# Linear attention and a mixture of experts on one core: zero fills copied in memory, weight preparation re-spaced, some row normalisation moved to ScalarE

## The chip, the core and the metric

The kernel runs on one core of a Trainium2 chip. The metric is the device time of one execution in microseconds (us), a median over several runs. A core has a matrix engine (TensorE, PE in the profile), a vector engine (VectorE, DVE), a scalar engine (ScalarE, ACT), a general engine (GpSimd, POOL) and an engine that mostly issues transfers (SyncE, SP). Each works through its own instructions in order and waits on semaphores that others raise. Transfers are moved by 16 DMA engines; in this kernel they are issued from SP's queue (hardware-generated, q1 in the profile) and from POOL's (software-generated, q0).

## The reference

The input is x with 2048 rows of 512 columns. Cut to what matters:

```python
# attention, 32 heads of 64 columns
q = relu(ln(x) @ Wq); k = relu(ln(x) @ Wk); v = ln(x) @ Wv
kv = einsum('bhsd,bhse->bhde', k, v)
key_sum = k.sum(axis=2)
out = einsum('bhsd,bhde->bhse', q, kv) / clip(einsum('bhsd,bhd->bhs', q, key_sum), 1e-6)
x = x + out @ Wo + bo
# experts: 8, the best 2 of each row, hidden width 352
scores = ln(x) @ gate_w.T + gate_b + bias
gates = softmax(top_2(scores))
h = silu(einsum('td,ehd->teh', ln(x), w1) + b1)
x = x + sum over the row's 2 experts of gate * (h @ w2 + b2)
```

`ln` subtracts the mean of a row and divides by the square root of its variance plus 1e-5.

## The kernel before, in words

Rows come in 16 tiles of 128 (`NT`), the 2048 inner columns of the attention in four quarters of 512 (`NQ`). A wide product is split for precision: every operand is held as a rounded upper half and the rest (`split`, L163 and 164: a cast on ScalarE, then a subtraction on VectorE unless another engine is named), and `mm3` (L156) makes three matmuls of each product.

**First half, `a_step(s)`, s = 0 to 63, quarter j and row tile t.** `a_k` makes k for one row tile (12 matmuls, a relu on ScalarE, two VectorE operations, one of which adds to the key sum `kacc`); `a_g` multiplies it by the normalised rows of the step before (12 matmuls) into four accumulators. In the first quarter the rows are also loaded, normalised (`norm`, L218), transposed and split, one row tile ahead of `a_k` (`a_norm`), and written to memory (`xnd`); in later quarters `a_xn` reads them back. At t = 2 of the next quarter `a_kv` turns the accumulators into the quarter's kv matrix, stores it (`kvd`), and makes the key sums for all partitions (`ksb`). The first half also prepares weights with `raw_load` (an SP load into a ring of four buffers) and `raw_split` (the cast and the subtraction): the next quarter's k weights, four parts at t = 9 to 12; this quarter's v weights, four parts at t = 13 and 14; in the last quarter the first q weights at t = 10 to 13; and all of w1 in 22 parts, one in each of the steps 16 to 37, staged and written to memory as `w1d`. Some subtractions of the first quarter are put on POOL.

**Second half, s = 0 to 63 again.** `b_q` makes q (12 matmuls and a relu), `b_n` divides by the key-sum product, `b_t` transposes, `b_o` multiplies by the quarter's matrix M = kv @ Wo (12 matmuls, `po`), and `b_add` adds to the row kept in memory (`x1d`). `b_w` and `b_m` build the next quarter's M in four parts, and wq parts are split at t = 5 to 8. `b_x1` loads a row two steps ahead; in the first quarter POOL adds `bo`. At step 1 of the second half the last kv matrix is made and stored, read back and turned into M before the first `b_o`. In the last of these quarters the rows are normalised again, scored, and scattered by expert into the table `xs_d` (blocks of 128 rows of 515 words).

**Zeros.** `xs_d` must hold zero rows, with -1 and a row number beside them, wherever no row is scattered: 136 blocks written by `b_fill` in the second half, three a step, from two SBUF buffers, plus 7 spare blocks. The 31 blocks of `out` after the result's own rows must be zero too, since rows for the second expert are added there. In the first quarter POOL issues those 31 blocks, the spare blocks, and a copy of three experts' w2 to memory (`w2d`); all of these go through `Late` (L600), which lets them start after the relu of step 1.

**Experts.** 37 tiles of gathered rows (`c_x` loads, `c_t` transposes and splits, `c_h` first product, `c_ht` transposes, `c_y` second product). `y_out` scales by the gate on ScalarE into a buffer of the same ring of four that `raw_load` uses, and POOL scatters and adds it to `out` in memory. When all tiles that could hold second-expert rows of a row tile are through (`last_of`, plus a lag of two), `merge(t)` adds that block of `out` to the result's rows, memory to memory; what isn't merged by the end is merged after the last tile.

**Order.** From the second half's last quarter on the program's order on TensorE, VectorE, ScalarE and SP is the written one (`manual_schedule`). Before that a scheduler orders the instructions by simulated times, and `hold(held, behind)` (L166) makes instructions start only after another has ended; `k_done[s]` is the relu of `a_k(s)`, `q_done[s]` that of `b_q(s)`.

Of the kernel before, what the change touches and what calls it, by code (L numbers as in the profile page):

```python
# [26 lines left out]
def linear_attention__then__moe_kernel(  # L27
# [113 lines left out]
    xs_d = dram.tile([(NB + SPARE) * P, CX], FP, name="xs_d")  # L141
    xs_b = xs_d.rearrange("(b p) c -> b p c", p=P)
    hd = dram.tile([NTT, P, HF], FP, name="hd")
    E2 = 3
# [73 lines left out]
    def norm(xt, dst):  # L218
        sm = const.tile([P, 16], FP, tag="sm", bufs=3, name="sm")
        st, mv, sd, rs = sm[:, 0:6], sm[:, 6:8], sm[:, 8:9], sm[:, 9:10]  # L220
        first = nc.vector.bn_stats(st, xt)
        nc.vector.bn_aggr(mv, st)
        root = nc.scalar.activation(sd, mv[:, 1:2], AF.Sqrt, bias=eps)
        nc.vector.reciprocal(rs, sd)
        last = nc.vector.tensor_scalar(dst, xt, mv[:, 0:1], rs, ALU.subtract, ALU.mult)
        return first, root, last
# [84 lines left out]
    def a_kv(j):  # L311

        for p0 in range(0, PP, 2):
            pkv = aux_bank("pkv").rearrange("p (a l b) -> p a l b", a=2, l=2)
            for p in range(p0, p0 + 2):
                for c in range(CC):
                    w, g = slot_n[0][:, c], slot_n[1][:, c]
                    nc.tensor.matmul(
                        pkv[:, p - p0], w[:, 0, ts(p, P)], g[:, :, ts(p, P)],
                        start=c == 0, stop=False,  # L320
                    )
                    nc.tensor.matmul(
                        pkv[:, p - p0, 0, :], w[:, 1, ts(p, P)], g[:, 0, ts(p, P)],
                        start=False, stop=c == CC - 1,
                    )
# [12 lines left out]
        ksb[j] = fpb.tile([P, QW], FP, tag="ksb", bufs=NQ, name="ksb")  # L338
        nc.scalar.copy(ksb[j], pks)
# [3 lines left out]
    q_done = {}  # L343

    def b_x1(s):
        j, t = divmod(s, NT)
        x1s[s] = fpb.tile([P, C], FP, tag="x1", bufs=4, name="x1")
        if j == 0:
# [3 lines left out]
            nc.gpsimd.tensor_add(x1s[s], x1s[s], bo_b)  # L352
# [147 lines left out]
    zeros = []  # L500

    def b_fill(s):

        if s == 0:
            for _ in range(2):
                zeros.append(temp())
                for i0, i1, v in ((0, C + 1, 0.0), (C + 1, C + 2, -1.0)):
                    hold([nc.gpsimd.memset(zeros[-1][:, i0:i1], v)], q_done[s])
        e, k = divmod(s, -(-SB // 3))
        rows = zeros[e % 2]  # L510
        if k == 0:
            to = float(2 * S + (SPARE + e) * P)
            nc.gpsimd.tensor_scalar(rows[:, C + 2 : CX], part, to, None, ALU.add)
        for n in range(3 * k, min(3 * k + 3, SB)):
            hold([nc.gpsimd.dma_start(xs_b[e * SB + n], rows)], q_done[s])  # L515
# [21 lines left out]
    n_w1 = W1N // 512  # L537
    NC = 2
    k_done = {}

    def a_step(s):
# [11 lines left out]
        if t == 8 and j + 1 < NQ:  # L553
            for c in range(CC):
                hold([raw_load(("k", j + 1, c), wk[ts(c, P), ts(j + 1, QW)])], k_done[s - 1])
        if t in (9, 10, 11, 12) and j + 1 < NQ:
            c = t - 9
            w = slot_s[(j + 1) % 2]
            raw_split(
                ("k", j + 1, c), w[:, c, 0, :], w[:, c, 1, :], nc.vector if j else nc.gpsimd  # L560
            )
        if t == 9 and j == NQ - 1:
            for c in range(CC):
                raw_load(("q", 0, c), wq[ts(c, P), ts(0, QW)])
        if t in (10, 11, 12, 13) and j == NQ - 1:
            c = t - 10
            raw_split(("q", 0, c), slot_s[0][:, c, 0, :], slot_s[0][:, c, 1, :])
        if t == 12:
            for c in range(CC):
                raw_load(("v", j, c), wv[ts(c, P), ts(j, QW)])  # L570
        if t in (13, 14):
            for c in (2 * t - 26, 2 * t - 25):
                raw_split(
                    ("v", j, c), slot_n[0][:, c, 0, :], slot_n[0][:, c, 1, :],
                    nc.vector if j else nc.gpsimd,
                )

        w = s - NT
        if 0 <= w < n_w1:
            if w == 0:  # L580
                hold([raw_load(("w1", 0), w1[:, ts(0, 512)])], k_done[s - 1])
# [3 lines left out]
            if w + 1 < n_w1:  # L585
                hold([raw_load(("w1", w + 1), w1[:, ts(w + 1, 512)])], k_done[s - 1])
# [3 lines left out]
        if j and t == 2:  # L590
            a_kv(j - 1)

# [71 lines left out]

    zero = temp()
    pool.memset(zero[:, 0 : C + 1], 0.0)
    pool.memset(zero[:, C + 1 : C + 2], -1.0)
    for b in range(NT + NZ):
        pool.dma_start(out[S + b * P : S + (b + 1) * P, :], zero[:, 0:C])
    for b in range(SPARE):  # L670
        pool.tensor_scalar(zero[:, C + 2 : CX], part, float(2 * S + b * P), None, ALU.add)
        pool.dma_start(xs_b[NB + b], zero)
    for e in range(E2):
        pool.dma_start(w2d[e, 0:HF].bitcast(FP), w2[e])
        pool.dma_start(w2d[e, HF : HF + 1].bitcast(FP), b2[e : e + 1, :])
# [23 lines left out]

    for s in range(NC, NQ * NT):  # L700
        a_step(s)
    b_x1(0)
# [156 lines left out]
    for s in range(NS - NT):  # L859
# [4 lines left out]
        b_fill(s)  # L864
# [16 lines left out]
        if t == 4:  # L881
# [9 lines left out]
        if t in (10, 11, 12, 13):  # L891
            b_w(j + 1, t - 10)
            b_m(j + 1, t - 10)
# [190 lines left out]
    for i in range(H1):  # L1084
# [38 lines left out]
    last_of = {  # L1123
        t: max(min(F1 + 2 * t + E, 2 * (G1 - 1) + E), 2 * t + E) for t in range(NT)
    }
# [27 lines left out]
    for n, i in enumerate(y_order):  # L1153
# [5 lines left out]
        if n == H1 - 1:  # L1159
            c_h(H1)  # L1160
            c_next(H1 + 2)
# [4 lines left out]
    for i in range(H1, NE):  # L1166
# [78 lines left out]
```

## Time and profile before

| | |
|---|---|
| runs shown (3) | 1022.0 to 1026.01 us, median 1024.93 us |
| the profiled execution | 1016.79 us, of which the span is 1015.1 us |
| mean granted TensorE clock | 0.993 of full speed |
| first half, second half, experts (about) | 0 to 393, 393 to 830, 830 to 1015 us |
| DMA, mean | 210 GB/s; SP's queue 129.83 MB, POOL's 82.19 MB |
| POOL, fills of `xs_d` in the second half (L515) | 136 issues, 545 ns each |
| POOL, zero blocks of `out` (L600) | 31 issues, 557 ns each |
| ScalarE, casts of weight parts (L164) | 86, 621 ns each |
| VectorE, their subtractions (L164) | 77, 708 ns each; 9 more on POOL, 1286 ns each |
| VectorE, normalising a row (L225) | 16, 652 ns each |
| ScalarE, a row with scale and bias (L243) | 16, 816 ns each |

The profile is one execution recorded by the hardware. A row of a group gives how many instructions it has and the mean duration of one; a timeline row gives start, duration, engine, line and operation, and in brackets how long the engine sat idle before it and what ended that. A row of busy time by stretches gives for each engine the busy microseconds and the number of instructions. Matmuls of TensorE overlap, so their durations add up to more than their time: distances from start to start and counts say how fast it goes.

### The profile page before, as it was taken

What the parts mean: (1) busy time and instruction counts of PE and PEld (TensorE: products, weight loads), DVE (VectorE), ACT (ScalarE), POOL (GpSimd) and SP (SyncE); (2) the same over time, 40 slices, a digit from 0 to 9 for tenths busy, and PEclk for the clock granted to TensorE, in tenths of its full rate; (3) what the DMA queues carried; (4) which work ended last, traced back from release to release, by engine and by line L of the source; (5) the groups of instructions that cost most, each with busy time, mean ns of one, the idle gap of its engine ahead of it and who ended that gap; (6) DMA issues with size and microseconds to landing.
All of it is one profiled execution on the core that took longest, in us unless ns stands there. A gap on an engine that the chain in (4) does not pass through costs nothing. (4 is left out here: it accounts for less than half of the span.)

```text
span 1015.1 us, 14856 instructions
## 1 busy us (share of the span) xinstructions
PE 987.5 (97%) x4902; PEld 823.7 (81%) x4902; DVE 560.2 (55%) x1380; ACT 344.7 (34%) x677; POOL 260.8 (26%) x357
## 2 busy tenths in 40 slices
PE   8999999999999999999999999999999999999994
PEld 5878887788888888788788888887888789889993
DVE  7864434453344226758756775675777777223331
ACT  4333323232123113313212322132544557444441
POOL 3643200000000013244312331221223220643354
PEclk9999999999999999999999999999999999999997
DMA  7984768765434236967866766587566597965788
GB/s 233 393 323 175 228 239 270 268 231 174 155 128 170 86 130 202 252 188 231 282 213 217 250 240 200 189 261 270 187 231 220 166 335 250 169 112 106 128 150 139
DMA packets 87884, 212.99 MB, mean 210 GB/s; under 512 B 11497, under 2 KB 14857, under 8 KB 87761
## 3 DMA queue, kind: packets, MB, share of 16 engines
q1 hardware_dynamic: 61984, 129.83, 38.9%
q0 software_dynamic: 25824, 82.19, 28.6%
q8 instruction: 43, 0.70, 0.3%
q14 instruction: 33, 0.26, 0.1%
HBM read 106.87 MB, written 111.47 MB: 215 GB/s over the span
## 5 line engine op out<-in xcount | busy, mean ns | idle before, releaser
L515 POOL DMA_DIRECT2D xs_d<-temp x136 | 73.5, 545 | 143.2 <-ACT q L362 125.0
L284 DVE SCALAR_TENSOR_TENSOR k<-pk,k 128x512 fp32r<-128x512 f32 x64 | 44.0, 688 | 118.1 <-ACT k L283 118.1
L158 PE MATMUL po<-area,qT 128*128 128x512 f32 x256 | 102.3, 399 | 2.4 <-ACT qT L164 2.4
L158 PE MATMUL pq<-area 128*128 128x512 f32 x256 | 103.3, 404 | 0.0
L158 PE MATMUL pk<-area 128*128 128x512 f32 x256 | 101.8, 398 | 0.9 <-ACT area L164 0.9
L160 PE MATMUL pk<-area 128*128 128x512 f32 x256 | 100.7, 394 | 0.9 <-DVE area L164 0.8
L160 PE MATMUL pq<-area 128*128 128x512 f32 x256 | 101.1, 395 | 0.0
L159 PE MATMUL g<-k,xn_hl 128*128 128x512 f32 x256 | 100.7, 393 | 0.3
L159 PE MATMUL pq<-area 128*128 128x512 f32 x256 | 100.9, 394 | 0.0
L159 PE MATMUL po<-area,qT 128*128 128x512 f32 x256 | 100.5, 392 | 0.0
L160 PE MATMUL g<-k,xn_hl 128*128 128x512 f32 x256 | 99.8, 390 | 0.0
L159 PE MATMUL pk<-area 128*128 128x512 f32 x256 | 99.7, 389 | 0.0
L160 PE MATMUL po<-area,qT 128*128 128x512 f32 x256 | 99.4, 394 | 0.1
L164 ACT CAST qT<-qtp 128x512 fp32r<-128x512 f32 x64 | 36.7, 587 | 178.6 <-PE qtp L249 178.6
L164 DVE TENSOR_TENSOR area<-raw,area 128x512 fp32r<-128x512 f32 x77 | 53.9, 708 | 73.5 <-ACT area L164 64.9
L158 PE MATMUL g<-k,xn_hl 128*128 128x512 f32 x256 | 91.1, 394 | 2.4 <-ACT k L283 2.4
L164 ACT CAST area<-raw 128x512 fp32r<-128x512 f32 x86 | 53.1, 621 | 116.4 <-DMA raw<-in_w 56.8
L352 POOL TENSOR_TENSOR x<-x,bo_b 128x512 f32<-128x512 f32 x16 | 21.1, 1326 | 275.1 <-DMA x<-in_x 265.8
L1134 POOL DMA_INDIRECT out<-ys,dest x37 | 58.4, 1577 | 109.3 <-ACT ys L1131 60.3
L283 ACT ACTIVATE k<-pk 128x512 fp32r<-128x512 f32 x64 | 38.3, 598 | 124.5 <-PE pk L160 124.4
L413 DVE TENSOR_TENSOR x<-x,po 128x512 f32<-128x512 f32 x48 | 32.9, 686 | 54.7 <-PE po L160 50.3
L362 ACT ACTIVATE q<-pq 128x512 f32<-128x512 f32 x64 | 38.4, 600 | 63.4 <-PE pq L160 39.4
(224 smaller groups left out, 2126.9 us busy)
## 6 DMA issues: line engine op xcount, KB each, us to landing
xs_d<-temp POOLq DMA_DIRECT2D x143, 257.5 KB, 4.7
xn_hl<-xnd SPq DMA_DIRECT2D x48, 512.0 KB, 4.8
x1d<-x SPq DMA_DIRECT2D x48, 256.0 KB, 3.7
x<-x1d SPq DMA_DIRECT2D x48, 256.0 KB, 4.1
w1d<-area SPq DMA_DIRECT2D x44, 256.0 KB, 4.1
area<-w1d POOLq DMA_DIRECT2D x16, 704.0 KB, 6.8
xg<-xs_d SPq DMA_DIRECT2D x37, 257.5 KB, 3.8
xnd<-xn_hl SPq DMA_DIRECT2D x16, 512.0 KB, 7.0
```

The source lines that it names most:

```text
L158: first = nc.tensor.matmul(o, lh, rh, start=start, stop=False)
L159: nc.tensor.matmul(o, lh, rl, start=False, stop=False)
L160: nc.tensor.matmul(o, ll, rh, start=False, stop=stop)
L164: return nc.scalar.copy(hi, src), on.tensor_sub(lo, src, hi.bitcast(FP))
L283: relu = nc.scalar.activation(k[:, 0, :], pk, AF.Relu)
L284: nc.vector.scalar_tensor_tensor(k[:, 1, :], pk, 0.0, k[:, 0, :].bitcast(FP), ALU.max, ALU.subtract)
L352: nc.gpsimd.tensor_add(x1s[s], x1s[s], bo_b)
L362: q_done[s] = nc.scalar.activation(q, pq, AF.Relu)
L413: nc.vector.tensor_add(x1, x1, pos.pop(s))
L515: hold([nc.gpsimd.dma_start(xs_b[e * SB + n], rows)], q_done[s])
L1134: added[i] = nc.gpsimd.indirect_dma_start(out[:, :], bass.IndirectOffsetOnAxis(dest[:, i : i + 1].bitcast(U32), 0), ys, None, compute_op=A ...
```

## The change

- `b_fill` no longer writes from SBUF. 15 blocks of zero rows (8 for the experts, 7 spare) and one 256 KB block of plain zeros are written to memory once, and the 136 blocks of `xs_d` and the 31 of `out` are copied from those, memory to memory, four a step, held behind POOL's own addition to the row two steps ahead (behind the relu of q from where there is none).
- The 15 + 1 blocks and the w2 copies are issued one job a step from step 32 of the first half, held behind the relu of that step, no longer in the first quarter.
- Weight parts: w1's 22 parts go to step 15 and to t = 1 to 7 of the three later quarters. k's parts go to t = 6 to 9 in the first quarter and 10 to 13 later (the first q parts likewise), loaded one and two steps ahead. v's parts go one to a step: t = 11 to 14 in the first quarter, from 14 on into the next quarter's t = 0 and 1 in the second and third, two a step at 14 and 15 in the last. All subtractions are on VectorE but one at the start.
- Rows 6 to 15 are normalised by ScalarE.
- The key sums are made at t = 6 (`a_ks`), no longer with `a_kv`.
- In the second half wq loads are issued at t = 3 (4 before) and M's parts made at t = 11 to 14 (10 to 13 before).
- Expert rows are loaded three tiles ahead from tile 16 on, every third into the ring that `y_out` uses. `last_of` is lowered for the early row tiles, and merges are made one a step, two from tile 32, none at the last but one.

```diff
-    xs_d = dram.tile([(NB + SPARE) * P, CX], FP, name="xs_d")
+    xs_d = dram.tile([(NB + NZ) * P, CX], FP, name="xs_d")
+    zero_d = dram.tile([P, C], FP, name="zero_d")
...
-        last = nc.vector.tensor_scalar(dst, xt, mv[:, 0:1], rs, ALU.subtract, ALU.mult)
+        if on_scalar:
+            nc.vector.scalar_tensor_tensor(nr, mv[:, 0:1], -1.0, rs, ALU.mult, ALU.mult)
+            last = nc.scalar.activation(dst, xt, AF.Identity, bias=nr, scale=rs)
+        else:
+            last = nc.vector.tensor_scalar(dst, xt, mv[:, 0:1], rs, ALU.subtract, ALU.mult)
...
-        ins = norm(xs.pop(t), xn)
+        ins = norm(xs.pop(t), xn, t > 5)
...
         words(nc.sync, kvd[j], kvt)
+    def a_ks(j):
         pks = aux_bank("pks")
...
-        for n in range(3 * k, min(3 * k + 3, SB)):
-            hold([nc.gpsimd.dma_start(xs_b[e * SB + n], rows)], q_done[s])
+    def b_fill(n):
+        if n < NB:
+            return nc.gpsimd.dma_start(xs_b[n], xs_b[NB + SPARE + n // SB])
+        to = S + (n - NB) * P
+        return nc.gpsimd.dma_start(out[to : to + P, :], zero_d)
...
+    w1_steps = [
+        s for s in range(NT - 1, NQ * NT) if s == NT - 1 or 1 <= s % NT < 8
+    ]
+    v_steps = {}
+    for j in range(NQ):
+        for c in range(CC):
+            s = 11 + c if j == 0 else 14 + c if j + 1 < NQ else 14 + c // 2
+            v_steps.setdefault(j * NT + s, []).append((j, c))
...
+        t_k = 10 if j else 6
+        if t == t_k - (2 if j else 1):
             for c in range(CC):
+                src = wk[ts(c, P), ts(j + 1, QW)] if j + 1 < NQ else wq[ts(c, P), ts(0, QW)]
+                hold([raw_load(("s", j, c), src)], k_done[s - 1])
+        if t_k <= t < t_k + CC:
+            c = t - t_k
...
+        if t == (11 if j else 10):
             for c in range(CC):
                 raw_load(("v", j, c), wv[ts(c, P), ts(j, QW)])
+        for jv, c in v_steps.get(s, ()):
+            raw_split(("v", jv, c), slot_n[0][:, c, 0, :], slot_n[0][:, c, 1, :])
+        if s in w1_steps:
+            w = w1_steps.index(s)
             raw_split(("w1", w), stage[:, 0, :], stage[:, 1, :])
...
+        if s + 1 in w1_steps:
+            w = w1_steps.index(s + 1)
+            hold([raw_load(("w1", w), w1[:, ts(w, 512)])], k_done[s - 1])
...
+        if j and t == 6:
+            a_ks(j - 1)
...
-    for b in range(NT + NZ):
-        pool.dma_start(out[S + b * P : S + (b + 1) * P, :], zero[:, 0:C])
...
+    later = [
+        (zero_block,), *((zero_rows, b) for b in range(NZ)), *((copy_weights, e) for e in range(E2))
+    ]
     for s in range(NC, NQ * NT):
         a_step(s)
+        if s >= 2 * NT and later:
+            job, *of = later.pop(0)
+            hold(job(*of), k_done[s])
...
-        elif RAW0 <= i < H1 + 2:
+        elif RAW0 <= i < H1 + 2 or i >= H1 + 4 and (i - H1) % 3 == 1:
...
-        b_fill(s)
+        for n in range(4 * s, min(4 * s + 4, NB + NT + NZ)):
+            hold([b_fill(n)], x1_in[s + 2] if s + 2 in x1_in else q_done[s])
...
+        if s == 6:
+            a_ks(NQ - 1)
...
-        if t == 4:
+        if t == 3:
             for c in range(CC):
                 raw_load(("q", j + 1, c), wq[ts(c, P), ts(j + 1, QW)])
...
-        if t in (10, 11, 12, 13):
-            b_w(j + 1, t - 10)
-            b_m(j + 1, t - 10)
+        if t in (11, 12, 13, 14):
+            b_w(j + 1, t - 11)
+            b_m(j + 1, t - 11)
...
-        if i + 2 < NE:
-            c_x(i + 2)
+        if i + 3 < NE:
+            c_x(i + 3)
...
-    last_of = {
-        t: max(min(F1 + 2 * t + E, 2 * (G1 - 1) + E), 2 * t + E) for t in range(NT)
-    }
+    last_of = {t: max(F1 + E - 1, 2 * t + E) for t in range(NT)}
...
-        for t in due[:2]:
+        for t in due[: 0 if i == NE - 2 else 2 if i > NE - 6 else 1]:
```

More of the change, by code (lines that the diff above doesn't have):

```diff
@@ L215, in linear_attention__then__moe_kernel, with norm @@
     load_x(1)
-    def norm(xt, dst):
+    def norm(xt, dst, on_scalar):
         sm = const.tile([P, 16], FP, tag="sm", bufs=3, name="sm")
-        st, mv, sd, rs = sm[:, 0:6], sm[:, 6:8], sm[:, 8:9], sm[:, 9:10]
+        st, mv, sd, rs, nr = sm[:, 0:6], sm[:, 6:8], sm[:, 8:9], sm[:, 9:10], sm[:, 10:11]
         first = nc.vector.bn_stats(st, xt)
@@ L342, in linear_attention__then__moe_kernel @@
     qs, qTs, x1s, xn2s, x2Ts, ms, pos, pgs = {}, {}, {}, {}, {}, {}, {}, {}
-    q_done = {}
+    x1_in, q_done = {}, {}
     def b_x1(s):
@@ L351, in b_x1 @@
                 hold([load], k_done[NQ * NT - 4])
-            nc.gpsimd.tensor_add(x1s[s], x1s[s], bo_b)
+            x1_in[s] = nc.gpsimd.tensor_add(x1s[s], x1s[s], bo_b)
         else:
@@ L498, in at_place @@
         return bass.IndirectOffsetOnAxis(place[:, t, n : n + 1].bitcast(U32), 0)
[L500 to L513, printed above, removed]
-        for n in range(3 * k, min(3 * k + 3, SB)):
-            hold([nc.gpsimd.dma_start(xs_b[e * SB + n], rows)], q_done[s])
+    def b_fill(n):
[3 more added lines that the diff above has]
+        return nc.gpsimd.dma_start(out[to : to + P, :], zero_d)
     idle = fp1.tile([P, CX], FP, tag="f1", bufs=F1B, name="idle")[:, 0 : C // 2].bitcast(BF)
@@ L537, in linear_attention__then__moe_kernel @@
     n_w1 = W1N // 512
+    w1_steps = [
+        s for s in range(NT - 1, NQ * NT) if s == NT - 1 or 1 <= s % NT < 8
+    ]
+    assert len(w1_steps) == n_w1
+    v_steps = {}
[3 more added lines that the diff above has]
+            v_steps.setdefault(j * NT + s, []).append((j, c))
     NC = 2
@@ L551, in a_step @@
             a_xn(s + 1)
-        if t == 8 and j + 1 < NQ:
+        t_k = 10 if j else 6
+        if t == t_k - (2 if j else 1):
             for c in range(CC):
-                hold([raw_load(("k", j + 1, c), wk[ts(c, P), ts(j + 1, QW)])], k_done[s - 1])
-        if t in (9, 10, 11, 12) and j + 1 < NQ:
-            c = t - 9
+                src = wk[ts(c, P), ts(j + 1, QW)] if j + 1 < NQ else wq[ts(c, P), ts(0, QW)]
+                hold([raw_load(("s", j, c), src)], k_done[s - 1])
+        if t_k <= t < t_k + CC:
+            c = t - t_k
             w = slot_s[(j + 1) % 2]
[L559 to L568, printed above, removed]
+            raw_split(("s", j, c), w[:, c, 0, :], w[:, c, 1, :])
+        if t == (11 if j else 10):
             for c in range(CC):
                 raw_load(("v", j, c), wv[ts(c, P), ts(j, QW)])
[L571 to L581, printed above, removed]
+        for jv, c in v_steps.get(s, ()):
+            raw_split(("v", jv, c), slot_n[0][:, c, 0, :], slot_n[0][:, c, 1, :])
+        if s in w1_steps:
+            w = w1_steps.index(s)
             raw_split(("w1", w), stage[:, 0, :], stage[:, 1, :])
@@ L584, in a_step @@
                 words(nc.sync, w1d[l][:, ts(w, 512)], stage[:, l, :])
-            if w + 1 < n_w1:
-                hold([raw_load(("w1", w + 1), w1[:, ts(w + 1, 512)])], k_done[s - 1])
+        if s + 1 in w1_steps:
+            w = w1_steps.index(s + 1)
+            hold([raw_load(("w1", w), w1[:, ts(w, 512)])], k_done[s - 1])
         k_done[s] = a_k(s)
@@ L663, in linear_attention__then__moe_kernel @@
     place = const.tile([P, NT, 2], I32, name="place")
-    zero = temp()
-    pool.memset(zero[:, 0 : C + 1], 0.0)
-    pool.memset(zero[:, C + 1 : C + 2], -1.0)
-    for b in range(NT + NZ):
-        pool.dma_start(out[S + b * P : S + (b + 1) * P, :], zero[:, 0:C])
[L670 to L675, printed above, removed]
     gb = temp()[:, 0 : 2 * E].rearrange("p (l e) -> p l e", l=2)
@@ L698, in linear_attention__then__moe_kernel, with zero_block, zero_rows, copy_weights @@
     pool.memset(area[:, 80 * KB : 84 * KB].bitcast(FP), 0.0)
+    zero = temp()
+    pool.memset(zero[:, 0 : C + 1], 0.0)
+    pool.memset(zero[:, C + 1 : C + 2], -1.0)
+    def zero_block():
+        return [nc.gpsimd.dma_start(zero_d, zero[:, 0:C])]
+    def zero_rows(b):
+        to = float(2 * S + b * P)
+        return [
+            nc.gpsimd.tensor_scalar(zero[:, C + 2 : CX], part, to, None, ALU.add),
+            nc.gpsimd.dma_start(xs_b[NB + b], zero),
+        ]
+    def copy_weights(e):
+        return [
+            nc.gpsimd.dma_start(w2d[e, 0:HF].bitcast(FP), w2[e]),
+            nc.gpsimd.dma_start(w2d[e, HF : HF + 1].bitcast(FP), b2[e : e + 1, :]),
+        ]
+    later = [
+        (zero_block,), *((zero_rows, b) for b in range(NZ)), *((copy_weights, e) for e in range(E2))
+    ]
     for s in range(NC, NQ * NT):
         a_step(s)
+        if s >= 2 * NT and later:
+            job, *of = later.pop(0)
+            hold(job(*of), k_done[s])
+    assert not later
     b_x1(0)
@@ L1160, in linear_attention__then__moe_kernel @@
             c_h(H1)
-            c_next(H1 + 2)
+            c_t(H1 + 2)
+            for k in (4, 5):
+                c_x(H1 + k)
             c_ht(H1)
```

## The prediction

> **What bounds the kernel.** I read the page first, then busy time by stretches of 25 us, then the timelines of TensorE and ScalarE around every stretch that is short of matmuls.
>
> ```profile
> span 1015.1 us, 14856 instructions
> PE 987.5 (97%) x4902; PEld 823.7 (81%) x4902; DVE 560.2 (55%) x1380; ACT 344.7 (34%) x677; POOL 260.8 (26%) x357
> ```
>
> TensorE is busy 97% of the span, and the diff leaves its arithmetic alone. So only its stalls, its slow clock and the tail after it can be won or added to. Busy time hides part of a stall, since matmuls overlap; the counts in brackets do not:
>
> ```profile
> 150.00:175.00 25.00, 24.85 (x107) 19.40 (x106) 10.42 (x16) 7.57 (x13) 0.00 (x0) 1.00 0.82 248
> 175.00:200.00 25.00, 23.47 (x99) 18.03 (x98) 12.18 (x19) 7.46 (x13) 0.00 (x0) 1.00 0.83 284
> 225.00:250.00 25.00, 25.00 (x111) 20.50 (x110) 7.18 (x12) 4.86 (x9) 0.00 (x0) 1.00 0.52 178
> ```
>
> The columns are the engines in the order PE, PEld, DVE, ACT, POOL, then clock, DMA share and GB/s. An undisturbed stretch of full-width matmuls has 111, so one takes 25/111 = 0.225 us; the first two stretches lack 4 and 12, **3.6 us**. The TensorE timeline shows where, and ScalarE's shows why:
>
> ```profile
> 176.09 0.39 PE L160 MATMUL pk<-area 128*128 128x512 f32 x1
> 177.20 0.73 PE L158 MATMUL g<-k,xn_hl 128*128 128x512 f32 x2 [0.72 <-ACT k L283]
> ```
> ```profile
> 175.38 1.28 ACT L164 CAST area<-raw 128x512 fp32r<-128x512 f32 x2 [0.74 <-DMA raw<-in_wv]
> 176.56 0.59 ACT L283 ACTIVATE k<-pk 128x512 fp32r<-128x512 f32 x1
> ```
>
> TensorE waits for the relu of the row; the relu stood in ScalarE's queue behind weight casts, and these behind a load. That happens where a k or v part and a w1 part share a step. At 225 to 250 us there is one w1 part in each step and nothing is lost.
>
> The other losses, read alike (a start-to-start distance less the normal one):
> - 66.5 to 71 us, first quarter: 1.16, 0.52 and three of 0.34 us where 0.23 is normal, **1.6 us** (VectorE late with a transposed row behind a weight cast on ScalarE).
> - 414 to 421 us, entry of the second half:
>
> ```profile
> 413.94 0.60 PE L249 MATMUL qtp<-ident,qn 128*128 128x128 f32 x4
> 416.45 0.50 PE L158 MATMUL po<-area,qT 128*128 128x512 f32 x1 [1.91 <-ACT qT L164]
> ...
> 418.13 0.63 PE L159 MATMUL pq<-area 128*128 128x512 f32 x1
> 418.56 0.63 PE L160 MATMUL pq<-area 128*128 128x512 f32 x1
> ```
>
>   Four transposes take 0.43 us, so po could start at 414.37: 2.1 us lost. After it matmuls start 0.43 us apart for 3.1 us, another 1.6: **3.7 us**.
> - 484 to 485.4 us: 0.67, 0.34, 0.51, 0.34 us, **0.9 us**, behind a cast that waited 5.34 us for a wo load.
> - The tail: TensorE ends at 1001, the span at 1015.1; the chain of waits holds one scatter-add of 5.63 us where these land in 4.9 as a median and 4.5 at best.
>
> All of that is 3.6 + 1.6 + 3.7 + 0.9 = 9.8 us before the tail.
>
> On the second half of the 414 loss the Trainium skill ("TensorE: Matmul & The Clock Gate", Part 1) says the clock halves only after an idle activity window of about 3.4 us. Here a gap of about 2.1 us was followed by a halved clock; by the rule the gap would have cost 2.1, by the row it cost 3.7.
>
> **Part by part.**
>
> *Weight parts one to a step, w1 apart.* The casts and subtractions stay as many; eight subtractions of the first quarter move from POOL (1.286 us) to VectorE (0.708). From the second quarter on, w1 goes to t = 1 to 7, k (in the last quarter q) to 10 to 13, v from 14 on; loads run at least a step ahead. The four loads of a quarter's k or q leave SP together at t = 8, 4 x 0.33 = 1.3 us of issue, and the row reload behind them is read a step later. Only v's last parts, at t = 0 and 1 of the next quarter, meet a w1 part, and its loads are then three steps old. By the stretch at 225 us such steps lose nothing: **-3.6**. If that cover failed, each of the 4 + 4 parts of a quarter would cost the 1.1 - 0.2 = 0.9 us seen at 176.
>
> *Rows normalised by ScalarE, t > 5.* Ten times VectorE loses 0.652 (L225) and gains a one-column operation, 0.16 (rows of that size). ScalarE gains one full-row scale-and-bias, 0.816 by its own such row (L243). A row costs VectorE now 0.69 + 0.18 + 0.16 + 0.65 + 0.76 + 0.68 + 0.69 + 0.68 = 4.49; then 4.0, and 4.7 with a weight part. ScalarE goes from 2.1 to 3.5, the part's cast included. TensorE's row is 24 x 0.228 + 4 x 0.108 = 5.9. Both fit. bn_stats of the next row now waits for ScalarE; behind it on VectorE stand the k lower halves. The slack is the time from a normalised row's end to its transposes: 5.1 us at row 6 (31.45 to 36.57), 14 at row 12. Bounds: 0, and ten losses of 0.9, +9; I take **+0.5**, near zero as the slack is over ten times the added 0.3 us.
>
> *Zeros out of the first quarter.* 31 zero blocks, 7 row blocks and 6 weight copies leave 18 to 103 us, where from 28 to 58 us the DMA share is 1.01 and wk loads take 10.0 us to land against 3.4 for w1. Here k is asked at t = 5 and split from 6 (before: 8 and 9), a lead of 5.9 us. With loads in time, VectorE's delay at 66 goes: **-1.6** (bounds 0 and -1.6). Sixteen blocks and the weight copies come back at s = 32 to 50, one job a step: at most 0.58 us of POOL issue and 0.21 of arithmetic per block, on an engine that is at 0.00 there. They wait for relus; behind them on POOL stands only x1's addition, which sat idle 251 us. DMA there is at 0.41 to 0.54, and 16 x 0.73 + 3 x 2.3 = 19 us over 19 steps of 5.5 add 0.18. Cost nothing; uncovered, the 0.9 of a late load.
>
> *Memory to memory in the second half.* Price of a block from SBUF, from the DMA view of 500 to 600 us (49 blocks); price of a copy, from that of 18 to 28 us (three 704 KB copies, 2.11 of the 2.17 MB):
>
> ```profile
> q0 software_dynamic: 3920, 12.92, 35.9%
> ```
> ```profile
> q0 software_dynamic: 144, 2.17, 69.2%
> ```
>
> 35.9/49 = 0.73 us of all engines; 6.9/3 = 2.3 us per 704 KB, so 0.84 for 257.5 KB. Before, 136 x 0.73 = 99 us over 48 steps, 2.1 a step; after, 167 x 0.84 = 140 over 42 steps, 3.4 a step of some 6.4: the share of about 0.65 rises to 0.85. So copying is no saving in transfer. It frees SBUF buffers, and POOL stops waiting for them (26.1 us in six waits); its four issues of 0.55 a step, 2.2 us, delay only the x1 addition, wanted two steps later. It is covered by loads being early: wq is asked at t = 3 and split from 5, wo asked at 9 and split from 11, so two steps, 12 us, against landings of 4.5. That second step also takes the stall at 484: **-0.8** of 0.9.
>
> The Trainium skill ("DMA: Bandwidth & Descriptors", Queues, rings and completion order) speaks against this: an engine drains a whole packet of one queue before it turns to the next, so long pieces hold up the loads. The w2d copies of the trace moved in 48 packets of 45,056 bytes, and the loads landing beside them at 18 to 28 us took 2.6 us (xt): no harm there. By the rule each of four copies could hold a load 0.84 us, 3.4 us in all, still under 12.
>
> *Entry of the second half.* ScalarE waited 2.70 us at 406 for kvd's store, which ran beside nine fills of 0.73. After, fills hang on POOL's own x1 additions, those of s = 0 and 1 being ready early, and the key sums (0.62 + 0.69 + 0.45 + 0.585, once a quarter) leave the step; at t = 6 nothing waits for them. Bounds 0 and -3.7; I take **-2.2**, most of it, since the halved clock goes with the gap.
>
> *Rows three ahead.* TensorE waited for a row once, 0.7 us, at the start, untouched: 0. Six rows take a buffer of the ys ring, leaving three for 4.9 us of landing at a 4.9 us step: 0, at worst the 2.0 us that ys waited once.
>
> *Merges spread.* As many, earlier, none at the step before last. The last scatter-add meets no backlog: 5.63 - 4.7: **-0.9** (bounds 0 and -1.1).
>
> Sum: -3.6 + 0.5 - 1.6 - 0.8 - 2.2 - 0.9 = -8.6. The profiled execution took 1016.79 (1015.1 span and 1.7 around it): 1008.2. The median shown is 8.1 above it; I carry that over: **1016.3**.
>
> **Rivals.** *The stalls are mostly kept* (hidden elsewhere, or another wait in their place): only -3.6, -0.8 and +0.5 come: 1021.0. For it: the entry is a chain of stores and loads. Against: its cause at 66 us is taken away.
> *More than the sum*: the timed runs' 8.1 us are stalls of the same kind. All of 9.8 + 1.1 and all of 8.1 gone is 1005.9; half of the latter, 1010.
> *Slower: the copies crowd the loads of the second half.* If a load lands later than its 12 us lead, ScalarE's queue stops at each of 8 parts in three quarters, 0.94 us each as at 484: +22.6, 1024.9 - 7.8 + 22.6 = 1039.7. For it: share 0.85, and the 10.0 us landings at share 1.01. Against: 10.0 is still under 12.
>
> **How the numbers follow.** A measurement of this kernel tells 0.5% from no change: under 1019.8 or over 1030.1. Forecast 0.53 (own range 1012 to 1019.8), more than it 0.09, both faster: 0.62. Stalls kept: 0.19, same. Slower: 0.19, most of it the rival named, some of it the upper bound of the normalised rows (1016.3 + 8.5 = 1024.8) together with kept stalls. The range 1008 to 1030 leaves out half of "more" and most of "slower".
>
> **What would show it.** Right: 111 matmuls in each 25 us of the second quarter, no half clock near 417, the last scatter-add under 5 us. Wrong: waits of ScalarE for wq or wo over 5 us, landings of raw loads over 10, transposes waiting for the ScalarE-normalised row.

## The result, and the profile after

The changed kernel takes 1036.06 us (median of 4 runs, 1032.99 to 1038.29) against 1025.47 for the kernel before on the same chip (4 runs, 1022.0 to 1027.77): a ratio of 1.0104 [1.0065, 1.0143]. **It is 1.0% slower**; 1016.3 was forecast, and the time lies outside the range. The rival that came in is the slower one, the copies that crowd the loads of the second half.

The page of the profiled execution (1032.99 us around a span of 1031.3):

```profile
span 1031.3 us, 14840 instructions
PE 994.0 (96%) x4902; PEld 828.1 (80%) x4902; DVE 553.5 (54%) x1388; ACT 351.5 (34%) x687; POOL 246.0 (24%) x354
PEclk9999999999999999998999999999999999999998
```

The matmuls are as many, 4902, and the span is 16.2 us longer. Every loss is therefore time in which TensorE stood or ran at a lower clock, and it can be found by counting. The table compares the start of the n-th matmul with that of the same one in the profiled execution before. A column that falls has gained there, one that rises has lost. Some of the experiments below stand beside it, so that they can be read by place. They are single profiles, some from other chips; the kernel of E7 shares its first half with the kernel before and still wanders by up to 1.3 us there, so differences of 1 us between two columns say nothing.

```
   n  (before at)   after     E3     E5     E6     E7     E8     E9    E12
 280    (65.3)      +0.25  +0.32  +1.65  +0.15  -0.12  +0.23  +1.74  +1.07
 300    (71.0)      -1.28  -1.21  +0.11  -1.38  +0.60  -1.31  +0.20  -0.46
 700   (157.0)      -1.35  -1.28  +0.06  -1.45  +0.59  -1.36  +0.15  -0.53
 900   (206.4)      -4.99  -4.91  -3.57  -5.08  +1.31  -4.99  -3.48  -4.17
1400   (313.6)      -4.93  -4.86  -3.52  -5.03  +1.31  -4.94  -3.43  -4.11
1500   (336.5)      -2.45  -2.79  -2.15  -3.38  +1.31  -4.94  -3.43  -4.11
1800   (401.6)      -2.47  -2.82  -2.23  -3.45  +1.27  -5.01  -3.50  -4.14
1900   (426.8)      -5.47  -5.30  -5.28  -5.63  -1.79  -7.48  -6.52  -6.14
2100   (469.0)      -5.51  -5.33  -5.29  -5.55  -1.85  -7.40  -6.44  -6.15
2200   (491.0)      +4.24  -3.64  -5.74  -6.00  -2.57  -7.85  -6.89  -4.36
2500   (554.8)     +10.11  -3.90  +6.93  -6.75  -3.21  -8.60  -3.77  -3.89
2600   (576.5)     +14.54  +3.33  +8.88  -6.54  -2.90  -8.39  -1.30  +4.08
3200   (704.3)     +15.02  +3.84 +10.54  -4.89  -2.92  -6.74  +0.34  +4.57
4901  (1000.8)     +16.73  +4.96  +9.89  -5.71  -1.42  -6.76  +0.77  +6.05
```

The changed kernel is 4.99 us ahead by the 900th matmul, loses 2.5 near 314 us, wins 3.0 at the entry of the second half, and loses 20.5 between matmul 2100 (-5.51) and matmul 3200 (+15.02). Nearly all of that goes in the three rows up to 2600.

**The second quarter** is as forecast. Its busy time by stretches, with the columns in the order PE, PEld, DVE, ACT, POOL, clock, DMA share, GB/s:

```profile
150.00:175.00 25.00, 25.00 (x111) 20.52 (x110) 10.52 (x17) 8.11 (x14) 0.00 (x0) 1.00 0.57 188
175.00:200.00 25.00, 25.00 (x111) 20.52 (x110) 8.73 (x14) 4.93 (x9) 0.65 (x1) 1.00 0.42 139
```

Both stretches have 111 matmuls, where the kernel before had 107 and 99.

**The second half**, the same view of the changed kernel:

```profile
440.00:480.00 40.00, 33.23 (x156) 27.03 (x154) 20.61 (x37) 7.08 (x13) 21.21 (x34) 0.98 0.82 268
480.00:520.00 40.00, 39.30 (x175) 32.29 (x176) 28.88 (x56) 12.56 (x23) 21.33 (x38) 0.94 0.94 319
520.00:560.00 40.00, 36.00 (x162) 29.09 (x161) 20.30 (x43) 6.21 (x11) 15.94 (x33) 0.96 0.92 321
```

Some 190 matmuls fit in an undisturbed 40 us here (E8 below); these have 156, 175 and 162, while DMA runs at 0.82 to 0.94. The list of TensorE's waits (total, times, longest) is headed by one that the kernel before doesn't have:

```profile
PE pm L159 <- DVE area L165: 7.5, 1, 7.5
PE po L161 <- DVE qT L165: 5.3, 3, 2.9
PE g L159 <- ACT k L288: 2.6, 3, 1.7
PE po L159 <- ACT qT L165: 2.1, 3, 1.2
```

Now follow the 7.5 us back through the timelines of the changed kernel (start, duration, engine, line, operation; in brackets the idle time before it and who ended it). TensorE:

```profile
472.84 0.39 PE L160 MATMUL pq<-area 128*128 128x512 f32 x1
480.70 0.79 PE L159 MATMUL pm<-area,kv_sb 128*128 128x512 f32 x1 [7.47 <-DVE area L165]
481.29 0.63 PE L160 MATMUL pm<-area,kv_sb 128*128 128x512 f32 x1
```

VectorE, which has to empty the bank of the product pm:

```profile
479.36 0.69 DVE L165 TENSOR_TENSOR area<-raw,area 128x512 fp32r<-128x512 f32 x1 [11.53 <-ACT area L165]
479.96 0.68 DVE L165 TENSOR_TENSOR area<-pm,area 128x512 fp32r<-128x512 f32 x1
```

ScalarE, for whose cast VectorE waits:

```profile
461.37 0.60 ACT L370 ACTIVATE q<-pq 128x512 f32<-128x512 f32 x1 [2.06 <-PE pq L161]
462.05 1.30 ACT L165 CAST area<-raw 128x512 fp32r<-128x512 f32 x2
478.71 0.62 ACT L165 CAST area<-raw 128x512 fp32r<-128x512 f32 x1 [15.36 <-DMA raw<-in_wq]
...
480.70 0.61 ACT L370 ACTIVATE q<-pq 128x512 f32<-128x512 f32 x1
```

SyncE, which issued the load that ScalarE waits for:

```profile
465.79 1.21 SPq L208 DMA_DIRECT2D raw<-in_wq  x2
```

And GpSimd, with what went out in front of that load:

```profile
461.29 1.29 POOL L360 TENSOR_TENSOR x<-x,bo_b 128x512 f32<-128x512 f32 x1 [2.10 <-DMA x<-in_x]
462.52 3.87 POOL L511 DMA_DIRECT2D xs_d<-xs_d  x8
466.41 1.31 POOL L360 TENSOR_TENSOR x<-x,bo_b 128x512 f32<-128x512 f32 x1
...
475.33 1.25 POOL L360 TENSOR_TENSOR x<-x,bo_b 128x512 f32<-128x512 f32 x1 [0.34 <-issue]
```

Three things are to be seen. Two wq casts stand together at 462.05; the load of the third part leaves only at 465.79, when those two have given their buffers back (VectorE's second subtraction ends at 464.9), and it has landed when ScalarE goes on at 478.71, 12.9 us later. The third cast stands *ahead* of the relu of q (480.70) and of the cast of qT, so one late load stops ScalarE, then VectorE, then TensorE. And sixteen copies went out between 462.5 and 475, behind two additions of x1 the first of which had waited for its own load. The copies had also piled up. GpSimd issued none between 373 and 425 us, as this row shows:

```profile
424.10 1.29 POOL L360 TENSOR_TENSOR x<-x,bo_b 128x512 f32<-128x512 f32 x1 [51.02 <-DMA x<-in_x]
```

Only 16 of the 167 copies were out by 440 us (40 in E3 and E8 below); the rest came in the steps behind.

The other two losses are smaller. The stops at 533 and 547 us stand behind rows that VectorE waited for (reloads from `x1d`; waits of 5.9, 4.3 and 4.1 us up to 547). The one at 584 stands behind the third wq cast of the next quarter, which starts at 584.10 for a load that SP issued at 575.7.

The DMA view of the changed kernel from 440 to 600 us gives the price of a copy:

```profile
q0 software_dynamic: 3761, 31.11, 55.5%
...
xs_d<-xs_d POOLq DMA_DIRECT2D x120, 257.5 KB
```

55.5% of 160 us is 88.8, over 120 copies 0.74 us each. That is less than the 0.84 estimated, and nearly the 0.73 that a block from SBUF took in the kernel before (500 to 600 us). There, 71 blocks went out from 440 to 600 us.

### The profile page after: what moved, and what is told of

Same layout as the page of the kernel before. It is cut to its first block, busy times and chain, and to the rows that moved or that the text cites. A ratio compares the mean times of both kernels' runs of the same rounds, so it can differ in the third digit from the quotient of the medians.

```text
span 1031.3 us, 14840 instructions
## 1 busy us (share of the span) xinstructions
PE 994.0 (96%) x4902; PEld 828.1 (80%) x4902; DVE 553.5 (54%) x1388; ACT 351.5 (34%) x687; POOL 246.0 (24%) x354
## 4 chain that ended last, share of the span: by engine, by line
PE 82%; DMA 9%; DVE 5%; ACT 2%; issue 1%; SPq 0%; POOLq 0%; POOL 0%; DVEq 0%; ACTq 0%
PE g L159 5%; PE g L160 5%; PE g L161 5%; PE pk L159 5%; PE pk L161 5%; PE pk L160 5%; PE po L161 5%; PE po L159 4%; PE pq L159 4%; PE po L160 4%; PE pq L161 4%; DMA x1d<-x 4%; PE pq L160 4%; PE py L159 2%; PE py L160 2%; PE py L161 2%
## 5 line engine op out<-in xcount | busy, mean ns | idle before, releaser
L165 DVE TENSOR_TENSOR area<-raw,area 128x512 fp32r<-128x512 f32 x85 | 57.5, 688 | 124.4 <-ACT area L165 124.3
L161 PE MATMUL po<-area,qT 128*128 128x512 f32 x256 | 101.3, 401 | 5.4 <-DVE qT L165 5.3
L159 PE MATMUL po<-area,qT 128*128 128x512 f32 x256 | 104.0, 406 | 2.1 <-ACT qT L165 2.1
L160 PE MATMUL po<-area,qT 128*128 128x512 f32 x256 | 101.9, 398 | 0.0
L511 POOL DMA_DIRECT2D xs_d<-xs_d x136 | 65.9, 490 | 71.7 <-ACT q L370 47.7
L161 PEld LDWEIGHTS po<-area,qT 128*128 128x128 f32 x256 | 48.9, 191 | 18.3 <-DVE qT L165 7.6
L159 PEld LDWEIGHTS po<-area,qT 128*128 128x128 f32 x256 | 49.0, 191 | 13.1 <-ACT qT L165 3.2
## 6 DMA issues: line engine op xcount, KB each, us to landing
xs_d<-xs_d POOLq DMA_DIRECT2D x136, 257.5 KB
xg<-xs_d SPq DMA_DIRECT2D x37, 257.5 KB
```

What stands on the lines that cost most here:

```text
L159: first = nc.tensor.matmul(o, lh, rh, start=start, stop=False)
L160: nc.tensor.matmul(o, lh, rl, start=False, stop=False)
L161: nc.tensor.matmul(o, ll, rh, start=False, stop=stop)
L165: return nc.scalar.copy(hi, src), on.tensor_sub(lo, src, hi.bitcast(FP))
L511: return nc.gpsimd.dma_start(xs_b[n], xs_b[NB + SPARE + n // SB])
```

## The experiments

Each ratio is against the kernel before on the same chip. Four theories were set against one another: **A**, the copies hurt as they are made of long pieces that hold up loads; **B**, there are too many a step; **C**, their holds on the x1 additions delay and bunch them; **D**, the casts stand in the wrong place on ScalarE.

**E1 and E2: the pieces.** E1 writes the same blocks at the same places from two SBUF buffers, as the kernel before did; E2 cuts the copies into pieces as long as those.

```diff
-            return nc.gpsimd.dma_start(xs_b[n], xs_b[NB + SPARE + n // SB])
+            e = n // SB
+            rows = zeros[e % 2]
...
+            return nc.gpsimd.dma_start(xs_b[n], rows)
...
```

> The changed kernel with one part undone: the 167 zero blocks of the second half are written from two SBUF buffers again, at the same places (four a step, the same waits). Theory A (the length of the pieces: memory-to-memory copies move in long packets, and SP's loads wait behind them): the loads of wq land in under 6 us, TensorE's waits between 440 and 600 us fall from about 20 us to under 4, and the time is 1016 to 1020. Theory B (the number: 167 blocks at four a step crowd the DMA engines whatever their source): the waits stay, 1031 to 1038. Theory C (the holds: copies hung on POOL's x1 additions come in bunches): the same as B, since the holds are kept.

Measured 1049.09 us (1047.52 to 1052.04), ratio 1.0273 [1.0235, 1.0311]: above every figure that was expected, under any of the theories.

```diff
-            return nc.gpsimd.dma_start(xs_b[n], xs_b[NB + SPARE + n // SB])
+            return nc.gpsimd.dma_start(xs_b[n], xs_b[NB + SPARE + n // SB], max_dma_last_dim=4120)
...
```

> The changed kernel, with the copies still from memory to memory but cut into pieces of 4120 bytes (4096 for the blocks of the result) where they move in 16 long pieces now. Theory A: as with SBUF sources, 1016 to 1022, and wq's loads land in under 6 us. Theory B: 1031 to 1038, as the bytes are the same. Theory C: 1031 to 1038. If reading and writing memory at once is what costs, and not the length, it also stays at 1031 to 1038 while the SBUF version is fast.

Measured 1041.25 us (1038.84 to 1041.7), ratio 1.0188 [1.0154, 1.0223], again above what was expected. The DMA views from 440 to 600 us, first of E2, then of E1:

```profile
q0 software_dynamic: 8998, 29.69, 60.6%
...
xs_d<-xs_d POOLq DMA_DIRECT2D x116, 257.5 KB
```
```profile
q0 software_dynamic: 8640, 28.48, 62.5%
...
xs_d<-temp POOLq DMA_DIRECT2D x109, 257.5 KB
```

More packets, fewer bytes and yet larger shares than after's 55.5%: a block took 0.84 us of all engines in E2 and 0.92 in E1, where it took 0.74 in the changed kernel. So in the crowded stretch the copy is the cheaper form too, which the 0.73 of the emptier kernel before hides. A falls: the long pieces are the better form, and memory to memory is better than SBUF.

**E3 and E4: the holds and the number.** E3 hangs every copy on the step's relu of q instead of the x1 addition two steps ahead. E4 keeps the holds, makes three a step, and moves 31 blocks of `out` into the first half behind the weight copies.

```diff
-            hold([b_fill(n)], x1_in[s + 2] if s + 2 in x1_in else q_done[s])
+            hold([b_fill(n)], q_done[s])
```

> The changed kernel with every copy of a step held behind the relu of that step's q, as the fills of the kernel before are, and not behind POOL's x1 additions. Theory C: no bunch of ten copies at 466 to 475 us, TensorE's waits at 473 us gone, 1020 to 1026. Theory A and B: the copies still come four at a time, and the waits move but stay: 1030 to 1040. At the entry of the second half (400 to 420 us) more copies stand beside kvd's store, so up to 4 us may come back there under all three.

Measured 1025.2 us (1021.43 to 1029.95), ratio 1.0018 [0.9992, 1.0044].

```diff
+        *((b_fill, NB + b) for b in range(NT + NZ)), *((zero_rows, b) for b in range(NZ)),
...
-        if s >= 2 * NT and later:
+        if s >= NT - 2 and later:
...
-        for n in range(4 * s, min(4 * s + 4, NB + NT + NZ)):
+        for n in range(3 * s, min(3 * s + 3, NB)):
```

> The changed kernel with three copies a step in the second half (136 blocks of the table, as before) and the 31 blocks of the result copied in the first half, one job a step from step 14, the copies of w2 first; still memory to memory, same holds. Theory B: the waits between 440 and 600 us fall by two thirds or more, 1018 to 1024. Theory A: they fall a little, as a bunch still holds up a load: 1026 to 1034. Under all, the 2.5 us lost at 313 us beside a w2 copy go.

Measured 1021.17 us (1015.24 to 1026.65), ratio 0.9985 [0.9957, 1.0014]. E4's weight copies go out at steps 14 to 16, so part of its gain is the loss near 314 us, which it doesn't have. So C holds, and B too: between matmuls 2100 and 3200, where the changed kernel loses 20.5 us, E3 loses 9.2 and E4 10.2 in the profiles. Either cure takes away about half, and neither all. The two aren't quite apart, as the hold also decides how many copies meet in one stretch: from 440 to 600 us the changed kernel issues 120, E3 102 and E4 93. Both still stop near 570 us, for 4.4 and 5.9 us and with a halved clock behind it, and there ScalarE waits for wq as in the changed kernel. From E3's list of waits:

```profile
ACT area L165 <- DMA raw<-in_wq: 32.1, 8, 12.0
```

A wait of 12.0 us, where the written lead is two steps of 6, means that the cast doesn't stand where the step asks for it. Counting, in the built programs, the relus of q ahead of each cast of the weights for the third (q2, o2) and fourth quarter (q3, o3) shows where it does stand:

```
             q2            o2            q3            o3
written  21 22 23 24   27 28 29 30   37 38 39 40   43 44 45 46
before   15 15 15 16   15 15 27 29   31 31 31 32   32 32 43 44
after    15 15 15 16   17 19 31 33   31 31 31 32   34 35 44 45
E5       21 22 23 24   27 28 29 31   37 38 39 40   43 44 45 47
```

The program is put in order by a scheduler. In both kernels it has pulled the casts of wq forward by six steps, to the boundary of the quarter, where the slot that they write is read for the last time; the loads of parts 3 and 4 then need the buffers of parts 1 and 2.

**E5, E6 and E7: the casts.** E5 is the changed kernel with the casts of wq and wo held behind the relu of q of the step before. E6 has this and E3's holds. E7 holds the casts in the kernel before.

```diff
+            hi, lo = raw_split(("q", j + 1, c), w[:, c, 0, :], w[:, c, 1, :])
+            hold([hi], q_done[s - 1])
...
+            b_w(j + 1, t - 11, q_done[s - 1])
```

> The changed kernel, with the casts of wq and wo parts in the second half held behind the relu of the step before the one in which they are written (t = 5 to 8, 11 to 14). Without that the scheduler has put the casts of the next quarter's q parts at the quarter's boundary (after relus 15 and 31), right behind loads that wait for a buffer. Theory D (the place of the casts: the copies only lengthen landings, and a cast standing directly behind its load in ScalarE's queue turns that into a stall): the waits at 473 and 584 us go, the time is 1016 to 1024. Theory C (bunched copies): rows that are late for VectorE (533 to 553 us, about 7 us) stay whatever the casts do. If copies alone decide, 1031 or more.

Measured 1026.22 us (1023.09 to 1034.23), ratio 1.0084 [1.0051, 1.0116], slower than the 1016 to 1024 of theory D.

> The same with every copy held behind the relu of its own step's q. Theories C and D together: both kinds of wait go, and what the first half won (about 3 us at its end, 5 with the entry) shows: 1016 to 1020. If the number of copies at four a step matters besides (theory B), rows stay late and it is 1021 to 1026.

Measured 1016.72 us (1011.02 to 1022.33), ratio 0.9986 [0.9956, 1.0015].

> The kernel before with only the casts held in the same way. Theory D gives it the 0.9 us at 484 and perhaps 0.4 at 684: 1022 to 1025, the same within the interval. If held casts cost something by themselves (a relu or a row behind them), 1026 or more.

Measured 1013.42 us (1010.91 to 1017.09), ratio 0.9958 [0.9937, 0.9979]. The kernel before has 1018.19 us on this chip, so this is a gain of 0.4%, where no difference beyond the interval was expected.

E5 is the instructive one. The stops at 473 and 584 us are gone, but one of 10.3 us at 533.6 has come. Two of its waits:

```profile
PE po L161 <- DVE qT L165: 12.6, 4, 9.9
...
DVE x L423 <- DMA x<-x1d: 34.3, 9, 9.6
```

Now it is the reload of a row that is late. GpSimd of E5 shows what went out ahead of it:

```profile
485.60 3.87 POOL L513 DMA_DIRECT2D xs_d<-xs_d  x8
...
495.62 3.87 POOL L513 DMA_DIRECT2D xs_d<-xs_d  x8
...
506.55 3.87 POOL L513 DMA_DIRECT2D xs_d<-xs_d  x8
...
512.83 0.98 POOL L513 DMA_DIRECT2D xs_d<-xs_d  x2 [2.40 <-DMA xs_d<-xs_d]
...
533.49 0.49 POOL L513 DMA_DIRECT2D xs_d<-xs_d  x1 [0.41 <-DMA xs_d<-xs_d]
```

First copies leave eight at a time, 10 to 11 us apart, each volley behind an x1 addition. From 512.8 to 544.7 us GpSimd works off what has piled up: 36 copies, many of them issued as soon as an earlier one is through, at a DMA share of 0.99. E6 issues 20 in that time, at 0.82. So the hold does harm in two ways: it bunches the copies, and it shifts those of the first steps into later ones. E6 cures both casts and copies: it loses 0.7 us between matmuls 2100 and 3200, and no stop of the second half remains.

**E8: E6 with the w2 copies moved.** What is left is the loss near 314 us, 2.5 us in the changed kernel and 1.7 in E6. ScalarE, GpSimd and SyncE of the changed kernel there:

```profile
310.14 0.62 ACT L165 CAST area<-raw 128x512 fp32r<-128x512 f32 x1 [8.70 <-DMA raw<-in_w]
```
```profile
301.73 0.49 POOL L705 DMA_DIRECT2D w2d<-in_w  x1 [3.94 <-ACT k L288]
```
```profile
302.61 0.41 SPq L208 DMA_DIRECT2D raw<-in_w  x1
```

A load of w1 is issued 0.9 us behind a weight copy and has landed when the cast starts, 7.5 us later. E8 puts the three weight copies into steps 28 to 30, where no w1 part is asked for.

```diff
+    weights = [(copy_weights, e) for e in range(E2)]
...
+        if 2 * NT - 4 <= s and weights:
+            job, *of = weights.pop(0)
+            hold(job(*of), k_done[s])
+        elif s >= 2 * NT and later:
```

> The second of these with the three copies of w2 (704 KB each) moved from steps 49 to 51 of the first half, where w1 parts are loaded, to steps 28 to 30, where none is. The 2 us lost at 313 us go: 2 us under the second kernel, 1014 to 1018. If that loss is not the w2 copy's, no difference.

Measured 1010.55 us (1010.13 to 1011.22), ratio 0.992 [0.9895, 0.9944]: **the fastest, and faster than both kernels**. It is 6.2 us under E6 on the same chip, more than the 1.7 to be won at that place. E6's runs spread from 1011.02 to 1022.33 and its profile is of one of the two fastest; what the slower ones lose was not seen. Its page, its stretches and ScalarE at the place of the 7.5 us stop:

```profile
span 1008.4 us, 14865 instructions
```
```profile
480.00:520.00 40.00, 40.00 (x191) 33.10 (x190) 29.02 (x55) 11.08 (x19) 18.59 (x36) 1.00 0.84 290
520.00:560.00 40.00, 40.00 (x191) 33.15 (x190) 23.17 (x45) 8.96 (x16) 10.00 (x22) 1.00 0.81 280
```
```profile
459.47 0.60 ACT L370 ACTIVATE q<-pq 128x512 f32<-128x512 f32 x1 [2.12 <-PE pq L161]
...
463.84 0.62 ACT L165 CAST area<-raw 128x512 fp32r<-128x512 f32 x1
...
468.87 0.60 ACT L370 ACTIVATE q<-pq 128x512 f32<-128x512 f32 x1 [2.19 <-PE pq L161]
...
470.04 0.62 ACT L165 CAST area<-raw 128x512 fp32r<-128x512 f32 x1
```

One raw cast to a step and none of them waits; 191 matmuls in each stretch at a DMA share of 0.81 to 0.84. The copies are as many as in the changed kernel over the whole half; from 440 to 600 us they are 108 where it has 120.

**E9 to E12: the parts of E8 by themselves.** E9 writes the blocks from SBUF as E1 does.

> The fastest kernel so far (casts held, copies behind the relu of their own step, w2 copies at steps 28 to 30; 0.992 of the kernel before) with its 167 blocks written from SBUF. With good pacing the source may matter little: a block costs 0.73 us of the engines from SBUF and 0.77 in memory, so 0.99 to 0.995. If memory to memory is a gain by itself (16 packets a block against 64, and no wait of POOL for a buffer before a row number is written), this is slower by 5 us or more: 0.997 and over, with rows (x1) that VectorE waits for.

Measured 1017.79 us (1014.66 to 1021.77), ratio 0.999 [0.9971, 1.0008]. The rows come late again:

```profile
DVE x L423 <- DMA x<-x1d: 26.8, 7, 6.6
```

So memory to memory, with its pace set right, is worth about 7 us (E10 has 1010.96 on the same chip). A block took 0.83 us of all engines from 440 to 600 us in E9 (54.1% for 104), 0.75 in E8 (50.5% for 108). GpSimd also waits 21.2 us for E9's two buffers, and that wasn't tried by itself. E10 has VectorE normalise all rows:

```diff
-        ins = norm(xs.pop(t), xn, t > 5)
+        ins = norm(xs.pop(t), xn, False)
```

> The same fastest kernel with all rows normalised by VectorE as before. If that part brings nothing (my sum gave it +0.5 us, a small cost), the time is the same or half a microsecond less, and at the 300th matmul TensorE stands where it stands with it. If VectorE's relief is what removed the 1.6 us at 66 us, up to 1.6 us more, before the 300th matmul.

Measured 1010.96 us (1010.39 to 1011.54), ratio 0.9929 [0.9905, 0.9952], as E8 within the intervals: this part does nothing that can be told. E11 puts the experts' end back to that of before (rows two ahead, the old bounds, two merges a step):

```diff
-        if i + 3 < NE:
-            c_x(i + 3)
+        if i + 2 < NE:
+            c_x(i + 2)
...
-        for t in due[: 0 if i == NE - 2 else 2 if i > NE - 6 else 1]:
+        for t in due[:2]:
```

> The same fastest kernel with the experts' end as before: rows two tiles ahead, the old bounds and two merges a step. My sum gave this part 0.9 us, all of it between the last matmul and the end: 14.3 us there as in the kernel before, against 13.5. If the spread merges brought nothing, no difference.

Measured 1011.9 us (1010.7 to 1020.21), ratio 0.9949 [0.9919, 0.9979]; the interval reaches E8's. Three of its 11 runs took 1017.8 to 1020.2, the others at most 1013.0. Its profile has TensorE wait for a gathered row at 980 us, as E8's doesn't:

```profile
PE xgtp L254 <- DMA xg<-xs_d: 1.0, 1, 1.0
```

That and a tail (from the last matmul to the end) of 14.7 us where E8 has 14.0 make some 2 us in the profiles. E12 is E8 without the held casts.

> The same fastest kernel without the held casts: the scheduler puts wq's casts at the quarters' boundaries again. Theory D: waits of ScalarE for wq of 10 us and more come back there, TensorE loses 3 to 8 us near 475 and 570, 0.995 to 1.000. If pacing the copies was all, no difference to 0.992.

Measured 1018.61 us (1012.91 to 1021.94), ratio 0.9991 [0.9969, 1.0014]. ScalarE of E12:

```profile
559.53 1.30 ACT L165 CAST area<-raw 128x512 fp32r<-128x512 f32 x2 [1.02 <-PE pq L161]
573.38 0.62 ACT L165 CAST area<-raw 128x512 fp32r<-128x512 f32 x1 [12.55 <-DMA raw<-in_wq]
```

The pair of casts and the wait behind it are back. D is worth some 7 us with the copies on the relus of q (0.9991 against 0.992).

## Why the prediction was wrong, point by point

- *Weight parts one to a step*, -3.6: measured -3.6 (-1.35 to -4.99 between matmuls 700 and 900), with 111 matmuls in both stretches. Right.
- *Rows normalised by ScalarE*, +0.5, and *zeros out of the first quarter*, -1.6: between matmuls 280 and 300, where the stall at 66 us stood, the changed kernel gains 1.5, and so do E3, E5, E6, E8, E9 and E12. (The columns of E5 and E9 start higher: those profiles ran 3.4 us at half clock near 8 us.) E10 gains the same 1.5 there, so the normalisation is about 0. Right in size; whether the zeros or the k parts' new places removed the stall isn't shown.
- *The blocks and weight copies that come back at s = 32 to 50*, "cost nothing; uncovered, the 0.9 of a late load": the mechanism was named, its size was not. It cost 2.5 at 314 us, since a w1 load stood right behind a weight copy for 7.5 us. E8, which moves the weight copies alone, and E4, which moves them too, don't lose it.
- **The failed step is the cover of the second half**: "It is covered by loads being early: wq is asked at t = 3 and split from 5, wo asked at 9 and split from 11, so two steps, 12 us, against landings of 4.5", with -0.8 for it. It measured +20.5. The lead was read off the written steps. In the built order the casts of wq stand at the boundary of the quarter, right behind the release of the buffers that their loads need; the lead is nothing but the landing itself, and ScalarE's queue is exposed to all of it. The profile of before held the hint: ScalarE waited 5.34 us, until 483.37, for a wo load that SP had issued at 476.94 at the earliest:

```profile
476.94 3.09 SPq L207 DMA_DIRECT2D raw<-in_wo  x3
```

  With the load asked at t = 9 and the cast written at 10, a step of some 6 us, a wait of 5.34 would need a landing of over 11 us; this one landed within 6.4. So the cast stood not where it was written, and the step by which the change would take "the stall at 484" wasn't there. E5, E6 and E12 show the cast's place to be a cause.
- A second fault lies in the same step. The copies were spread evenly in thought, "3.4 a step of some 6.4". The average share came out as forecast (55.5% + 31.3% by the two main queues, 0.87 where 0.85 was said), but the hold on the x1 additions keeps them back until 425 us and then sends them in volleys of 8 to 16. E3 shows what this does: with as many copies in all, 1.0104 falls to 1.0018, and the 20.5 us to 9.2. With the casts held alone they fall to 15.8 (E5), with both cures to 0.7 (E6).
- *Entry of the second half*, -2.2: measured -3.0 between matmuls 1800 and 1900. Right in kind. E7 has the same gain of 3 in the kernel before, by holding casts alone, so it isn't shown which part of the change brings it.
- *Rows three ahead*, 0, and *merges spread*, -0.9: the tail went from 13.9 to 13.4, half of what was forecast, and the chain of waits of the changed kernel ends in a scatter-add of

```profile
1018.91 4.70 DMA out<-ys,dest
```

  where it was 5.63. E11 adds that the rows three ahead spare TensorE about 1.3 us in a run without other stops; the 0 was low.
- *The 8.1 us between the profiled run and the median*: carried over. Here the profiled run lies 3.1 below the median. E8 and E10 spread over 1.1 us in five runs each, the kernel before over 11 to 12 in 25 and 27 runs on the same chips. But E11, with the same second half as E8, spread over 9.5 in 11 runs, so five runs may be too few to meet a slow one. That much of the 8.1 is stalls that differ from run to run, as a rival supposed, is likely, but it was not tried by itself.
- *The slower rival*, 22.6 for a load later than 12 us: the right place, but that its price is close to the 20.5 measured is luck. It was not 24 stops of 0.94 us but three stretches of 9.8, 5.9 and 4.4, the middle one for late rows and not for weights, and the point from which it decides is a few microseconds of landing, not 12.

Together: 1.35 + 3.6 + 3.0 + 0.5 = 8.5 us won, where the sum without the failed -0.8 has 7.8 (the entry gave more than forecast, the merges less); 2.5 + 20.5 lost at the two places, and 1.7 more between matmul 3200 and the end, not followed further: +16.2, the difference of the two profiled runs. E8's profiled run, on another chip, is 6.7 under that of before (1010.13 against 1016.79).

## What to carry to other kernels

Read the lead of a load from the order in which its reader was built or ran, not from the step that the source writes it in: a scheduler that pulls a cast to the first free slot turns an early load into one that an in-order engine waits for. Don't hang background transfers on an instruction that itself waits for a load they slow down; pace them by the engine that bounds the kernel. When a change moves much traffic, compare the start of the n-th matmul in the two traces first: gains and losses separate at once, and each loss has a place to look at.

## What the runs showed of the hardware

- A 257.5 KB copy from memory to memory moves in 16 packets of 16,480 bytes, from SBUF in 64 packets of 4,120 bytes. From 440 to 600 us, where the runs are crowded, a block took 0.92 us of all engines in E1 (SBUF, 109 blocks) and 0.84 in E2 (short pieces, 116), against 0.74 in the changed kernel (120 copies); in the kernel before, from SBUF, it took 0.73 (500 to 600 us, 49 blocks). The copy also makes the faster kernel: 1.0104 against 1.0273 bunched, 0.992 against 0.999 paced. The Trainium skill ("DMA: Bandwidth & Descriptors", Queues, rings and completion order) says that an engine drains a whole packet of one queue before it switches to another; from that one would expect long pieces to hold up the loads more, and these runs show the opposite order. Whether the shorter time on the engines is the whole reason was not found.
- With sixteen copies issued in 13 us beside it, a 256 KB load took 12.9 us to land; the median for wq in the kernel before was 4.5.
- After the 7.9 us gap at 472.8 TensorE ran at half clock from 478.3 to 485.1, after a 3.2 us gap that ended at 550 for 3.4 us. A gap of 2.07 us (start to start) at 313.5 was followed by full clock, though one of 2.18 at 414 in the kernel before was followed by half clock: the length of the gap alone doesn't decide. The place may: in the changed kernel the clock falls at 478.32, 550.00 and 587.55 and rises at 485.15, 553.42 and 590.96, and all these lie whole multiples of 3.413 us apart. On this grid the gap at 313.5 is cut by an edge at 314.48, while the one at 414 lies within one step (413.78 to 417.19, counted back from the fall at 417.19). No run moved a gap on purpose to try it.
